# Saturating addition for the sampling coordinates of a deformable convolution, in place of an addition with a pointer scalar and a separate clip

## The chip, the cores and the metric

The kernel runs on one core of one Trainium2 chip. The core has five engines that work side by side, each from its own in-order list of instructions: TensorE (PE in the profile, with its weight loads as PEld), VectorE (DVE), ScalarE (ACT), GpSimd (POOL) and SyncE (SP), which here only starts DMA transfers. Engines wait for each other through semaphores. The metric is the time of one execution on the device in microseconds (us); lower is better. Before the change it is 9059.61 us, the median of three runs (9051.79, 9059.61 and 9065.78).

## What is computed

The input `x` is 16 images of 64 x 64 pixels with 128 channels. Layer 0 is a deformable sampling: a 3 x 3 convolution gives every channel and pixel two offsets, the offsets plus the pixel's own row and column are clipped to the image, and the normalized image is sampled there by bilinear interpolation. Layer 1 is an attention inside each token and a mixture of experts over 64 experts. Cut to the part that the change touches:

```python
offsets = conv(x, W) + b
off = offsets.transpose(0, 3, 1, 2).reshape(-1, h, w, 2)
coords = off.reshape(bc, -1, 2) + grid[None]
c0 = clip(coords[..., 0], 0, w - 1)
c1 = clip(coords[..., 1], 0, h - 1)
lt0, lt1, rb0, rb1 = floor(c0), floor(c1), ceil(c0), ceil(c1)
mapped = bilinear(xf, lt0, lt1, rb0, rb1, c0 - lt0, c1 - lt1)
```

## The kernel before

**Tiling.** An image is cut into eight chunks (`NCH`) of 8 columns x 64 rows, 512 pixels each. The 128 partitions hold channels. For a chunk the convolution runs on TensorE in two halves `s` (32 rows each), nine taps a half, into the PSUM tile `cbank` (128 x 512). For each half `coords(s)` turns the offsets in `cbank` into absolute coordinates in the SBUF tile `cd` (128 x 2 x 512: axis 0 is the row, axis 1 the column).

**From the coordinates to the sample.** `clip()` limits `cd` to 0..63, rounds the row coordinates to bfloat16 into `pc[:, 0]` on ScalarE, and sends the column coordinates to the DRAM buffer `cc_d` on SyncE's queue. `part2()` and `part3()` take the rounding's remainder twice (GpSimd and ScalarE), so that three bfloat16 numbers hold a row coordinate; `spread()` brings them by way of `pc_d` into the tile `parts`. All of this is for the next chunk. For the present chunk `sample()` takes two channels of each 32-channel group at a time (16 pairs `p` a chunk, each of two slots): `load_cols` broadcasts columns from `cc_d` into `chat` by DMA, `ramp_cols` makes a column weight of it on ScalarE, `spread_rows` broadcasts the row coordinates with bfloat16 matmuls into `yps` in PSUM, `ramp_rows` (ScalarE) makes `rhat` of it, `mains` multiplies with the image rows `xr` back into `yps`, `product` (VectorE) multiplies `yps` with `chat` into `prod`, and `sums` adds into `acc`. `tokens()` then runs a chunk's attention, whose large elementwise products (`sc`, `ev`) are on GpSimd, whose sums (`den`, `att`) are on VectorE, and whose exponentials are on ScalarE.

**Order.** Nothing is left to an automatic scheduler. `conv`, `sample`, `tokens`, `prep` and `tail` only record their operations with a slot (a due time; 32 slots a chunk). `Work.order()` then simulates the engines with the durations of `Work.duration()` and writes each engine's list: at every step, of the operations that are ready, the one with the smallest start plus 40 times its slot. `Work.duration()` charges a VectorE operation 145 ns + 1.045 ns an element + 30 ns for each pointer scalar, and a `tensor_scalar` from SBUF to SBUF 150 ns + 0.53 ns an element. [...] So a change in one operation's cost or kind alters the order of everything. `Work.emit()` (L200) issues the list; this is why almost all instructions carry line L204 in the profile, and why groups are told apart by the names of their tiles.

**Stages in time.** Image 0 runs alone; then a loop (L1271) of seven turns with two images each, whose work overlaps (while image b is sampled, the next one is normalized and the one before is finished); then image 15; then `general()`, which decides on a fallback for large offsets that these inputs don't take; then `finish()`, the experts and the output.

The two lines of `coords(s)` that make a coordinate, and the clip behind them:

```python
nc.vector.scalar_tensor_tensor(
    cd[:, 0], off[:, 0], cb, bcast(self.iot[:, 32 * s : 32 * (s + 1)], 2, SW),
    ALU.add, ALU.add)
...
nc.vector.tensor_scalar(self.cd, self.cd, 0.0, float(IMG - 1), ALU.max, ALU.min)
```

Here `cb` is a pointer scalar (one bias a partition) and `iot` a table 0..63. Behind the two coordinate operations of a half stands `far`, a reduction over the same `cbank`, after which TensorE may write `cbank` again.

Of the kernel before, what the change touches and what calls it, by code (L numbers as in the profile page):

```python
# [8 lines left out]

F32 = mybir.dt.float32  # L10
BF16 = mybir.dt.bfloat16
# [2 lines left out]
ALU = mybir.AluOpType  # L14
# [5 lines left out]
P = 128  # L20
B, IMG, C = 16, 64, 128
NPIX = IMG * IMG
NCH = 8
SW = IMG // NCH
# [23 lines left out]
def bcast(ap, axis, n):  # L48

    shape = list(ap.shape)  # L50
    return ap.unsqueeze(axis).to_broadcast(shape[:axis] + [n] + shape[axis:])
# [7 lines left out]
def by_columns(nc, out, weights, moving, start=True, stop=True):  # L59

    for c in range(0, out.shape[0], 32):
        nc.tensor.matmul(
            out[c : c + 32], weights[:, c : c + 32], moving, start=start, stop=stop)


def channel(t, v, m):

    a, h = divmod((v - m) % 4, 2)
    return 32 * m + 16 * a + 2 * t + h
# [87 lines left out]
class Work:  # L157
# [42 lines left out]
    def emit(self, ops):  # L200
        for op in ops:
            engine = getattr(self.nc, op.lane)
            for fn, args, kwargs in op.calls:
                getattr(engine, fn)(*args, **kwargs)  # L204

    def emit_in_order(self):
        self.emit(sorted(self.ops, key=lambda op: op.slot))
# [171 lines left out]
class Images:  # L379
# [8 lines left out]
    def __init__(self, ctx, tc, x, conv_w, conv_b, w_qkv, b_qkv, w_proj, b_proj, gate_w, gate_b,  # L388
# [3 lines left out]
        nc = tc.nc  # L392
# [30 lines left out]
        for v in range(4):  # L423
            for m in range(4):
                at, c = slice(32 * v + m, 32 * (v + 1), 4), channel(0, v, m)
                nc.scalar.dma_start(
                    self.cb[at], conv_b.rearrange("(c s) -> c s", s=2)[c : c + 15 : 2])
                for s in range(2):
                    engine = nc.vector if s else nc.gpsimd
# [44 lines left out]
        for r in range(2):  # L474
# [7 lines left out]
            for i, factor in enumerate((  # L482
# [3 lines left out]
        self.iot = keep([P, IMG], "iot")  # L486
        nc.gpsimd.iota(self.iot, [[1, IMG]], base=0, channel_multiplier=0,
                       allow_small_or_imprecise_dtypes=True)

# [10 lines left out]
        for g in range(4):  # L502
            for t in range(3):
                at = 32 * g + 8 * t
# [23 lines left out]
        for o in range(2):  # L528
# [5 lines left out]
            for g in range(4):  # L534
                for r in range(2):
                    at = 32 * g + 24 + r
# [31 lines left out]
        for m in range(4):  # L568
            nc.vector.memset(self.red[m], 0.0)
            for v in range(4):  # L570
                a, h = divmod((v - m) % 4, 2)
                at = 14 + 16 * a + h
# [211 lines left out]
    def conv(self, k, slot):  # L784
        plan = Work(self.nc, self.tc)
        nc = plan
        par, col = divmod(k, 4)

        def tap(s, t):
            kh, kw = divmod(t, 3)  # L790
            by_columns(
                nc, self.cbank, self.wconv[:, t, s, :],
                self.pad[:, kh + par : kh + par + 63 : 2, kw + 16 * col : kw + 16 * col + 16],
                start=(t == 0), stop=(t == 8))

        def coords(s):
            ps, hs = self.cbank, slice(256 * s, 256 * (s + 1))
            off = ps.rearrange("p (r w t) -> p t r w", w=SW, t=2)
            cd = self.cd[:, :, hs].rearrange("p t (r w) -> p t r w", w=SW)
            cb = self.cb[:, s : s + 1]  # L800
            nc.vector.scalar_tensor_tensor(
                cd[:, 0], off[:, 0], cb, bcast(self.iot[:, 32 * s : 32 * (s + 1)], 2, SW),
                ALU.add, ALU.add,
            )
            nc.vector.scalar_tensor_tensor(
                cd[:, 1], off[:, 1], cb, bcast(self.iot[:, SW * k : SW * (k + 1)], 1, 32),
                ALU.add, ALU.add,
            )
            nc.vector.tensor_reduce(
                self.far[:, 2 * k + s : 2 * k + s + 1], ps, AX.X, ALU.max,  # L810
                apply_absolute_value=True,
            )

        def clip():
            nc.vector.tensor_scalar(self.cd, self.cd, 0.0, float(IMG - 1), ALU.max, ALU.min)
            nc.scalar.copy(self.pc[:, 0], self.cd[:, 0])
            nc.sync.dma_start(self.cc_d[k % 2], self.cd[:, 1])

        def part2():
            nc.gpsimd.tensor_tensor(  # L820
                self.cd[:, 0], self.cd[:, 0], self.pc[:, 0], ALU.subtract)
            nc.scalar.copy(self.pc[:, 1], self.cd[:, 0])

        def part3():
            nc.gpsimd.tensor_tensor(
                self.pc[:, 2], self.cd[:, 0], self.pc[:, 1], ALU.subtract)

        def spread():
            for v in range(4):
                at = 32 * v  # L830
                nc.sync.dma_start(
                    self.pc_d[v].rearrange("o x n -> x o n"), self.pc[at : at + 32])
                nc.sync.dma_start(
                    self.parts[k % 2][at : at + 24].rearrange("p m n -> p (m n)"),
                    self.pc_d[v].rearrange("o (t m) n -> (o t) (m n)", t=8))


        for s, at in enumerate((range(5), range(12, 17))):
            for t in range(9):
                plan.together(slot + at[t // 2] + 0.5, lambda s=s, t=t: tap(s, t))  # L840
            plan.add(slot + at[-1] + 1, lambda s=s: coords(s))
        for i, fn in enumerate((clip, part2, part3, spread)):
            plan.add(slot + 18 + 2 * i, fn)
        return plan
# [640 lines left out]
```

## Time and profile before

The profile is of one execution, which took 9034.22 us by itself; its span (first to last instruction) is 9032.4 us, and 1.8 us lie around it. It is 0.28% below the median of the runs.

| what | value |
|---|---|
| median of three runs | 9059.61 us |
| the profiled execution's own time | 9034.22 us |
| its span | 9032.4 us |
| image 0, until the loop | 0 to 621 us |
| seven loop turns of two images | 621 to 7952 us, some 1047.8 us each |
| image 15 | 7952 to 8557 us |
| experts and output | 8557 to 9032 us |
| granted TensorE clock in the loop | 0.98 to 0.99 of full speed |
| coordinate additions (`cd<-cbank,cb,iot`) | 512 of 474 ns on VectorE |
| clips (`cd<-cd`) | 128 of 1002 ns on VectorE |

In the groups of instructions each row names the line, the engine, the operation, what it writes and reads, the shape and the count; behind the bar stand the busy time in us, the mean ns of one, and the idle time of the engine just before such instructions with what ended it. A row of the waits names who waited, for whom, the total us, how often, and the longest. A row of a stretch gives, for each engine, the busy us and, in brackets, the instructions.

### The profile page before, as it was taken

To read this page: it belongs to the slowest core of one execution; us is meant where nothing else is said; L and a number is where in the kernel's file an instruction comes from. 1 tells how busy PE (TensorE), PEld (TensorE's weight loads), DVE (VectorE), ACT (ScalarE), POOL (GpSimd) and SP (SyncE) were. 2 spreads that over 40 slices of the span, in tenths; PEclk is the share of its full clock that TensorE was granted. 3 is DMA by queue.
4 is the path that set the end of the run, shared out by engine and by line. 5 is a ranking of instruction groups with operands and counts; after the bars stand their busy time and mean duration, and the time that the engine had idled before them with its cause. 6 is when DMAs were issued, how large, how long until landed. Compare 5 with 4: busy or idle time off the path is not lost. (4 is left out here: it accounts for less than half of the span.)

```text
span 9032.4 us, 466631 instructions
## 1 busy us (share of the span) xinstructions
PE 8116.7 (90%) x205574; PEld 4234.7 (47%) x205574; DVE 7255.1 (80%) x10177; ACT 6550.6 (73%) x8082; POOL 7625.9 (84%) x5699
## 2 busy tenths in 40 slices
PE   6999999999999999999999999999999999999464
PEld 3544545454444545445454544445454544544234
DVE  3888888888888888888888888888878888888713
ACT  3777777777777878777777877778777877777400
POOL 1999998989999998989989899899989999899700
PEclk9999999999999999999999999999999999999656
DMA  5666666667666666667666766666676676666278
GB/s 140 189 180 182 192 183 184 191 187 194 176 188 177 194 184 191 186 179 197 181 185 180 196 191 179 184 179 193 181 195 181 184 198 175 185 177 185 78 238 295
DMA packets 1057495, 1678.72 MB, mean 186 GB/s; under 512 B 444272, under 2 KB 662128, under 8 KB 1051312
## 3 DMA queue, kind: packets, MB, share of 16 engines
q1 hardware_dynamic: 1033648, 1613.26, 63.9%
q8 instruction: 1615, 26.46, 1.3%
q10 hardware_dynamic: 21760, 35.14, 1.1%
q14 instruction: 472, 3.87, 0.2%
HBM read 1378.68 MB, written 268.96 MB: 182 GB/s over the span
## 5 line engine op out<-in xcount | busy, mean ns | idle before, releaser
L204 DVE SCALAR_TENSOR_TENSOR prod<-chat,yps 128x1024 f32<-128x1024 f32 x2048 | 2462.7, 1206 | 652.2 <-PE yps L204 142.0
L204 ACT ACTIVATE rhat<-yps 128x1024 f32<-128x1024 f32 x2048 | 2089.2, 1022 | 1153.8 <-PE yps L204 1004.6
L204 PEld LDWEIGHTS yps<-rhat,xr 32*32 32x32 f32 x131072 | 2174.8, 104 | 1385.3 <-ACT rhat L204 652.5
L204 PE MATMUL yps<-rhat,xr 32*32 32x176 f32 (+1 forms) x131072 | 2585.0, 275 | 199.6 <-ACT rhat L204 154.9
L204 POOL TENSOR_TENSOR ev<-sc,qkv 128x1024 f32<-128x1024 f32 x1019 | 2425.5, 2380 | 155.0 <-ACT sc L204 140.5
L204 PE MATMUL cbank<-pad,wconv 128*32 128x512 f32 x18432 | 2489.6, 617 | 49.1 <-DVE far L204 39.7
L204 POOL TENSOR_TENSOR sc<-qkv 128x1024 f32<-128x1024 f32 x1019 | 1980.1, 1943 | 46.3 <-POOLq L1271 7.5
L204 POOL TENSOR_TENSOR sc<-sc,top 128x1024 f32<-128x1024 f32 x1019 | 1993.7, 1958 | 20.2 <-ACT top L204 7.6
L204 DVE TENSOR_REDUCE den<-sc 128x64 f32<-128x1024 f32 x1024 | 1238.9, 1210 | 154.4 <-ACT sc L204 152.1
L204 ACT ACTIVATE chat<-chat,cbi,csc 128x1024 f32<-128x1024 f32 x1024 | 1265.0, 1239 | 108.7 <-DMA chat<-cc_d 100.1
L204 DVE TENSOR_REDUCE att<-ev 128x64 f32<-128x1024 f32 x1024 | 1237.3, 1208 | 103.3 <-POOL ev L204 73.9
L204 ACT ACTIVATE sc<-sc 128x1024 f32<-128x1024 f32 x1024 | 1078.1, 1053 | 198.6 <-POOL sc L204 149.1
L204 ACT ACTIVATE chat<-chat,cbi 128x1024 f32<-128x1024 f32 x1024 | 1159.0, 1142 | 25.0 <-DMA chat<-cc_d 23.7
L204 PE MATMUL acc<-prod,red 128*32 128x512 f32 x8192 | 1142.0, 617 | 20.7 <-DVE prod L204 19.2
L204 PE MATMUL yps<-parts,sel 32*32 32x512 bf16 x16384 | 926.2, 388 | 223.4 <-DVE prod L204 198.7
L204 PEld LDWEIGHTS cbank<-pad,wconv 128*32 128x32 f32 x18432 | 489.8, 109 | 891.9 <-issue 757.1
L204 PEld LDWEIGHTS <-sel 32*32 32x32 bf16 x16384 | 291.2, 88 | 1034.0 <-issue 993.4
L204 DVE RECIPROCAL den<-den 128x128 f32<-128x128 f32 x512 | 480.9, 939 | 7.7
L204 PE MATMUL bank<-wqkv,tr 128*32 128x384 f32 x4096 | 434.2, 495 | 17.1 <-DVE qkv L204 13.3
L204 DVE SCALAR_TENSOR_TENSOR qkv<-bank,rstd,bqkv 128x384 f32<-128x384 f32 x512 | 311.0, 607 | 108.5 <-PE bank L204 102.1
L204 POOL TENSOR_TENSOR att<-att,den 128x128 f32<-128x128 f32 x512 | 258.2, 504 | 120.7 <-DVE att L204 116.7
L204 POOL TENSOR_TENSOR qkv<-qkv,kmm 128x128 f32<-128x128 f32 x512 | 213.4, 417 | 157.9 <-DVE kmm L204 155.7
(166 smaller groups left out, 7629.2 us busy)
## 6 DMA issues: line engine op xcount, KB each, us to landing
chat<-cc_d SPq DMA_DIRECT2D x8192, 128.0 KB
xr<-xn_d SPq DMA_DIRECT2D x512, 128.0 KB
pc_d<-pc SPq DMA_DIRECT2D x512, 96.0 KB
parts<-pc_d SPq DMA_DIRECT2D x512, 96.0 KB
xl<-in_x_dram SPq DMA_DIRECT2D x128, 256.0 KB
xres<-in_x_dram SPq DMA_DIRECT2D x256, 128.0 KB
xn_d<-wt SPq DMA_DIRECT2D x128, 256.0 KB
cc_d<-cd SPq DMA_DIRECT2D x128, 256.0 KB
```

The source lines that it names most:

```text
L204: getattr(engine, fn)(*args, **kwargs)
```

## The change

A table `at` of grid plus bias is made once in the setup, one row of 64 for each of the two halves. A coordinate is then one operation: `cbank` plus the table, limited to 0..63 in the same instruction. [...] The clip is gone, and what followed it (the rounding to `pc`, the transfer to `cc_d`) now follows the coordinates directly. The planner knows the new call as `add_within` with two tensors and two constants, so it charges 145 ns + 1.045 ns an element and no pointer, and doesn't count it among the operations that it keeps apart from GpSimd's.

```diff
+                if fn == "add_within":
+                    out, a, b, lo, hi = args
+                    engine._custom_dve(TENSOR_ADD_SAT, out=out, in0=a, in1=b, s0=hi, s1=lo)
+                else:
+                    getattr(engine, fn)(*args, **kwargs)
...
+        self.at = keep([P, 2, IMG], "at")
+        for s in range(2):
+            nc.vector.tensor_scalar(
+                self.at[:, s], self.iot, self.cb[:, s : s + 1], None, ALU.add)
...
-            nc.vector.scalar_tensor_tensor(
-                cd[:, 0], off[:, 0], cb, bcast(self.iot[:, 32 * s : 32 * (s + 1)], 2, SW),
-                ALU.add, ALU.add,
-            )
-            nc.vector.scalar_tensor_tensor(
-                cd[:, 1], off[:, 1], cb, bcast(self.iot[:, SW * k : SW * (k + 1)], 1, 32),
-                ALU.add, ALU.add,
-            )
+            at = self.at[:, s]
+            for axis, grid in enumerate((
+                    bcast(at[:, 32 * s : 32 * (s + 1)], 2, SW),
+                    bcast(at[:, SW * k : SW * (k + 1)], 1, 32))):
+                nc.vector.add_within(cd[:, axis], off[:, axis], grid, 0.0, float(IMG - 1))
...
         def clip():
-            nc.vector.tensor_scalar(self.cd, self.cd, 0.0, float(IMG - 1), ALU.max, ALU.min)
             nc.scalar.copy(self.pc[:, 0], self.cd[:, 0])
             nc.sync.dma_start(self.cc_d[k % 2], self.cd[:, 1])
```

More of the change, by code (lines that the diff above doesn't have):

```diff
@@ L8 @@
 from concourse._compat import with_exitstack
+from concourse.dve_ops import TENSOR_ADD_SAT
 F32 = mybir.dt.float32
@@ L203, in emit @@
             for fn, args, kwargs in op.calls:
-                getattr(engine, fn)(*args, **kwargs)
+                if fn == "add_within":
[3 more added lines that the diff above has]
+                    getattr(engine, fn)(*args, **kwargs)
     def emit_in_order(self):
@@ L799, in coords @@
             cd = self.cd[:, :, hs].rearrange("p t (r w) -> p t r w", w=SW)
-            cb = self.cb[:, s : s + 1]
-            nc.vector.scalar_tensor_tensor(
-                cd[:, 0], off[:, 0], cb, bcast(self.iot[:, 32 * s : 32 * (s + 1)], 2, SW),
-                ALU.add, ALU.add,
-            )
-            nc.vector.scalar_tensor_tensor(
-                cd[:, 1], off[:, 1], cb, bcast(self.iot[:, SW * k : SW * (k + 1)], 1, 32),
-                ALU.add, ALU.add,
-            )
+            at = self.at[:, s]
[3 more added lines that the diff above has]
+                nc.vector.add_within(cd[:, axis], off[:, axis], grid, 0.0, float(IMG - 1))
             nc.vector.tensor_reduce(
```

## The prediction, made before the changed kernel ran

> **What bounds the kernel now.** I read the stretches first, one for each loop turn (second and third turn; the columns are PE, PEld, DVE, ACT and POOL busy, granted clock, DMA):
>
> ```profile
> 1669.00:2717.00 1048.00, 980.42 (x25508) 504.88 (x25504) 889.44 (x1240) 820.08 (x1013) 958.96 (x714) 0.98 0.67 187
> 2717.00:3764.00 1047.00, 979.64 (x25464) 505.04 (x25460) 887.23 (x1236) 814.61 (x1006) 953.48 (x710) 0.98 0.67 186
> ```
>
> PE is busy 93.5% of a turn, POOL 91%, DVE 85%. No engine is full: PE bounds, and loses 68 us of a turn to waits. Next the groups of PE in the turn from 1669 to 2717, for what ended those 68 us:
>
> ```profile
> L204 PE MATMUL yps<-rhat,xr 32*32 32x176 f32 (+1 forms) x16384 | 322.3, 275 | 24.8 <-ACT rhat L204 19.4 <-issue 4.5
> L204 PE MATMUL cbank<-pad,wconv 128*32 128x512 f32 x2324 | 315.2, 620 | 4.9 <-DVE far L204 4.7
> L204 PE MATMUL acc<-prod,red 128*32 128x512 f32 x1024 | 142.1, 616 | 2.2 <-DVE prod L204 2.2
> L204 PE MATMUL yps<-parts,sel 32*32 32x512 bf16 x2056 | 116.5, 388 | 27.3 <-DVE prod L204 24.6 <-PEq L1271 1.6 <-issue 0.7
> ```
>
> DVE ends 24.6 + 4.7 + 2.2 = 31.5 us of them. Third, DVE's groups, shapes kept apart:
>
> ```profile
> L204 DVE SCALAR_TENSOR_TENSOR prod<-chat,yps 128x1024 f32<-128x1024 f32 x2048 | 2462.7, 1206 | 652.2 <-PE yps L204 142.0 <-ACT sc L204 99.9 <-DMA chat<-cc_d 94.3
> ...
> L204 DVE SCALAR_TENSOR_TENSOR cd<-cbank,cb,iot 128x256 f32<-128x256 f32 x512 | 225.3, 474 | 87.3 <-PE cbank L204 87.1
> ...
> L204 DVE TENSOR_REDUCE far<-cbank 128x1 f32<-128x512 f32 x256 | 174.0, 680 | 0.0
> L204 DVE TENSOR_SCALAR cd<-cd 128x1024 f32<-128x1024 f32 x128 | 128.2, 1002 | 0.0
> ...
> L204 DVE TENSOR_TENSOR t<-bank,t 128x512 f32<-128x512 f32 x128 | 88.0, 688 | 85.0 <-PE bank L204 80.9 <-ACT sc L204 2.0 <-ACT chat L204 1.0
> ```
>
> The clip's mean of 1002 ns hides a spread, which the view of the tile `cd` gives (min/median/max), and the timeline around one clip shows why:
>
> ```profile
> L204 DVE TENSOR_SCALAR cd<-cd x128: 677/826/2769, 125.0 to 8367.5; 128x1024 f32<-128x1024 f32 x128
> ```
> ```profile
> 1584.14 2.38 POOL L204 TENSOR_TENSOR ev<-sc,qkv 128x1024 f32<-128x1024 f32 x1
> ...
> 1585.08 1.99 DVE L204 TENSOR_SCALAR cd<-cd 128x1024 f32<-128x1024 f32 x1
> ...
> 1586.48 0.85 POOL L204 TENSOR_TENSOR qkv<-qkv,kmm 128x128 f32<-128x128 f32 x1
> ```
>
> The clip begins beside POOL's `ev`, ends 0.55 us after it (1587.07 against 1586.52), and POOL's next instruction then takes 0.85 us where its group has 0.42: the two hold each other up.
>
> **Step 1, DVE's work.** The 128 clips go: 128.2 us, 16.0 in a turn. The 512 coordinate operations change kind. One of 512 elements reduced takes 680 ns, one of 1024 (`den`) 1210, so an element costs 1.035 ns and the 256 of `cd` 265; its fixed part is 474 - 265 = 209 ns. Without a pointer scalar the fixed part is 1206 - 1060 = 146 ns (`prod`) or 688 - 530 = 158 ns (`t`). The new operation should then take 411 to 423 ns; I take 417, 57 less, 29 us in all. This program of add, minimum and maximum is not in the trace. If it costs less than the rows say, I see no row under 411. Above stands RECIPROCAL, 939 ns for 128 elements, about 6.2 ns an element, which would make 1.74 us. MAX8 and MATCH_REPLACE8 (4411 and 4398 ns for 4096) and the batch-norm statistics (685 for 512) run about one element in 1.04 ns, so I go by those. The two operations for `at` (190 ns each by the `mats` row, 64 elements) fall near 15.6 us, before DVE idles 5.93 us for a transfer: nothing. DVE is freed of 128 + 29 = 157 us, 2.2% of 7255.
>
> **Step 2, POOL's work.** Sorting POOL's instructions by whether a clip ran beside them: 66 `att` take 763 ns against 466; 56 of `sc<-sc,top` 2197 against 1944; 23 of `sc<-qkv` 2069 against 1940; 7 of `qkv` 856 against 411. That is 19.6 + 14.2 + 3.0 + 3.1 = 40 us, 5 in a turn. The new operation reads PSUM and one SBUF table, as the old addition did, beside which I see no such lengthening.
>
> **Step 3, what reaches the end.** Low: the order stays as good and only work on the chain counts. I followed the chain back through six turns (from the last matmul, at idle time to the releaser, else to the instruction before). DVE is 16% of it, POOL 2.5%, the coordinate additions 8.1 us a turn, the clip never. 57/474 of 8.1 is 1.0 us. Of 423 waits of PE and PEld that DVE ended in seven turns, 14 had a clip in DVE's unbroken work before them, at most 8.4 us, so up to 1.2 a turn; half of it, 0.6, makes 1.6 a turn. With 16 images as eight turns: 13 us. High: queueing. DVE's busy share falls from 84.9% to 83.0%; if waiting goes as busy over free, 5.62 becomes 4.88, 13% less, 4.1 us of the 31.5, 33 us in eight turns, plus the 8 us of pointers: 41. Between: 27 us.
>
> **Step 4, what moves.** The instruction order of the changed kernel shows DVE's loop body at 1225 instead of 1241 instructions, PE's at the same work in another order. Cover on PE, as work by the rows' durations: between `mains` and the next `spread_rows` on the same `yps` median 2.4 us in both; between `spread_rows` and `mains` 1.54 and 1.55; between one half's last tap and the next half's first 4.2 before, 4.9 after. So no step loses its cover. SP's transfer to `cc_d` moves up past 2 to 21 `chat` loads, `parts` up to 7, the rounding on ACT 0 to 5 pairs, POOL's two remainders stay within a group. A new order has a price of either sign: the two images of a turn are the same work in two orders, and between the reductions `most` lie 519.5 and 526.8 us, the latter with 3.8 us of PE idle at the loop's edge. That leaves 3.5 us, 0.7%; for a mean of two, 0.5%: 45 us either way.
>
> [...] The removed wait of POOL is a row (763 against 466). [...]
>
> **Rivals.** (a) The relief goes further: DVE's lateness also stands behind the ramps (19.4 us a turn) and POOL's waits; a third of 31.5 goes, 10 us a turn: 80 us, 8980. (b) Nothing arrives: the clip is off the chain, PE's waits stay: 4 us or less, 9056. (c) Slower: SP is an in-order queue, and now stands at `cc_d` sooner, behind coordinates that DVE may do late, while `chat` loads queue behind it. For and against:
>
> ```profile
> SPq L204 <- DVE cd L204: 115.6, 90, 11.0
> ```
> ```profile
> ACT chat L204 <- DMA chat<-cc_d: 123.8, 141, 3.3
> ```
>
> SP waits here already, and late `chat` costs ACT 123.8 and DVE 94.3 us, 218 in all. If these rise by half, 109 us, and half of it reaches PE: 55 - 27 = 28 us slower, 9088. It decides from a rise of a quarter (54 us). Against it: the clip that went was part of SP's wait. (d) The new operation is dear: at two cycles an element 150 + 530 = 680 ns, the chain's 8.1 us grow by 3.5 a turn, 28 us, against 19 of the rest: 9069. It turns from 612 ns (19/65 over 474). At RECIPROCAL's rate it would be past 9200. That the clip isn't removed is excluded: the order has none.
>
> **How the numbers follow.** From the profiled 9034.2 the sum gives 9007; the median of the runs stands 25.4 us above it, so 9059.6 - 27 = 9033. A difference under 0.2% (18 us) can't be told from none. Chances: forecast 0.45, with its own spread 9005 to 9041; (a) 0.14; (b) 0.22; (c) 0.13; (d) 0.06, of which 0.01 at RECIPROCAL's rate. Faster 0.59, same 0.22, slower 0.19. The range reaches to (a) with the new order's spread and to (c), 8965 to 9095; the dearest end of (d) is left out.
>
> **What would show it.** Step 1: additions near 417 ns, DVE some 157 us lower. Step 2: `att` near 466 ns, POOL some 40 us lower. Step 3: PE's idle time in a turn from 68 to about 65 us, the waits on `prod` lower. For (c): SP's and ACT's waits for `cd` and `chat` higher. For (d): additions over 600 ns. I am wrong if the new order's own luck exceeds 45 us, or if PE's matmuls themselves change.

## The result: 0.31% slower

The changed kernel takes 9081.03 us (median of 9 runs, 9070.88 to 9090.23), the kernel before, run beside it, 9052.07 (9 runs, 9035.34 to 9065.78). The ratio is 1.0031, 95% interval 1.0021 to 1.0041: some 28 us slower, where 27 us faster was forecast. The profiled execution took 9082.71 us, 2.0 us above its span of 9080.7.

What was priced as an instruction of the change came out as priced. First the groups of DVE in the changed kernel, shapes kept apart (busy us, mean ns of one, idle before):

```profile
L209 DVE SCALAR_TENSOR_TENSOR prod<-chat,yps 128x1024 f32<-128x1024 f32 x2048 | 2464.5, 1207 | 738.1 <-PE yps L209 169.5 <-ACT chat L209 132.2 <-ACT xln L209 87.3
...
L207 DVE CUSTOM_DVE_ANT_1 cd<-cbank,at 128x256 f32<-128x256 f32 x512 | 196.9, 415 | 79.1 <-PE cbank L209 70.3 <-issue 8.4
...
L209 DVE TENSOR_REDUCE far<-cbank 128x1 f32<-128x512 f32 x256 | 174.1, 680 | 0.0
L209 DVE SCALAR_TENSOR_TENSOR big<-big,logits 64x512 f32<-64x512 f32 x128 | 128.9, 1058 | 0.8 <-ACT logits L209 0.6
...
L209 DVE TENSOR_TENSOR gmv<-gmv 128x1 f32<-128x1 f32 x32 | 50.5, 1579 | 1.3
L209 DVE TENSOR_TENSOR farthest<-farthest,most 128x1 f32<-128x1 f32 x16 | 28.6, 1786 | 0.5
```

The saturating addition takes 415 ns (forecast 411 to 423), there is no clip, and DVE's idle time before `prod` grew. But DVE's busy time fell by 78 us only, from 7255.1 to 7176.8, not by 157. Three rows (`big`, `gmv`, `farthest`) took part of it back, against these of the kernel before, which the prediction did not look at:

```profile
L204 DVE SCALAR_TENSOR_TENSOR big<-big,logits 64x512 f32<-64x512 f32 x128 | 108.2, 880 | 0.8 <-ACT logits L204 0.6
...
L204 DVE TENSOR_TENSOR gmv<-gmv 128x1 f32<-128x1 f32 x32 | 21.5, 673 | 1.1
L204 DVE TENSOR_TENSOR farthest<-farthest,most 128x1 f32<-128x1 f32 x16 | 18.6, 1166 | 0.5
```

20.7 + 29.0 + 10.0 = 60 us more, for the same instructions. The two `gmv` operations have one element a partition and belong to the group normalization of the next image (`group3`); they have two SBUF operands, and their durations range from 159 to 2065 ns.

Second, the stretches, as before one for a loop turn (PE, PEld, DVE, ACT, POOL, clock, DMA), of the changed kernel:

```profile
2725.00:3780.00 1055.00, 985.65 (x25472) 505.48 (x25472) 880.29 (x1221) 816.61 (x1008) 949.38 (x710) 0.98 0.67 185
3780.00:4835.00 1055.00, 986.02 (x25472) 506.86 (x25472) 879.49 (x1221) 816.63 (x1008) 948.91 (x711) 0.98 0.67 185
```

From the loop's branches a turn takes 1053.5 us, 1046.6 before (means of the last six turns; the 1047.8 above is 1 us too long): 6.9 us more. All seven turns together are 55 us longer, image 0 is 5.4 us shorter and what follows the loop 1.7, which makes the 48 us between the two profiled executions, so the loss lies in the loop alone. (Some 20 of these 48 us are the spread of runs: the medians are 29 us apart, and the profiled execution of before lies 18 under its median.) POOL's busy time in a turn is 6 us lower and DVE's 8, and both only wait longer. PE idles 70.0 us a turn, 67.5 before, and its busy time grew by 4.4 us with the same matmuls in another order.

Third, the groups of PE by what ended their idle time, over the six turns from 1674 to 7995 of the changed kernel:

```profile
L209 PE MATMUL yps<-rhat,xr 32*32 32x176 f32 (+1 forms) x98304 | 1927.8, 275 | 161.2 <-ACT rhat L209 136.8 <-issue 17.1
L209 PE MATMUL cbank<-pad,wconv 128*32 128x512 f32 x13824 | 1863.3, 618 | 18.0 <-DVE far L209 10.4 <-DVE prod L209 3.9 <-issue 3.4
...
L209 PE MATMUL yps<-parts,sel 32*32 32x512 bf16 x12288 | 708.6, 390 | 167.2 <-DVE prod L209 144.0 <-issue 10.8 <-PEq L1275 8.2
...
L209 PE MATMUL bank<-gmv,avg 128*32 128x2 f32 (+1 forms) x192 | 6.0, 184 | 33.0 <-DVE gmv L209 33.0
```

and of the kernel before, six turns from 1669 to 7945:

```profile
L204 PE MATMUL cbank<-pad,wconv 128*32 128x512 f32 x13824 | 1871.3, 618 | 30.4 <-DVE far L204 28.6 <-issue 0.5
...
L204 PE MATMUL bank<-gmv,avg 128*32 128x2 f32 (+1 forms) x192 | 5.7, 178 | 8.2 <-DVE gmv L204 8.2
```

The wait for `far` fell from 28.6 to 10.4 us. The wait for `gmv` rose from 8.2 to 33.0 and took back more than that. The timeline of the changed kernel around one `gmv` shows how:

```profile
1547.84 2.34 POOL L209 TENSOR_TENSOR ev<-sc,qkv 128x1024 f32<-128x1024 f32 x1
...
1548.77 3.32 DVE L209 TENSOR_TENSOR gmv<-gmv 128x1 f32<-128x1 f32 x2
1550.15 1.92 POOL L209 TENSOR_TENSOR sc<-sc,top 128x1024 f32<-128x1024 f32 x1
1552.01 1.21 DVE L209 SCALAR_TENSOR_TENSOR prod<-chat,yps 128x1024 f32<-128x1024 f32 x1
1552.14 0.29 PE L209 MATMUL bank<-gmv,avg 128*32 128x1 f32 x8 [3.71 <-DVE gmv L209]
```

Two operations of one element hold DVE for 3.32 us: the first takes 1431 ns and ends at 1550.20, 0.02 us after `ev` on POOL (1550.18), the second 1853 ns and ends at 1552.09, 0.02 us after `sc` (1552.07). PE stands 3.71 us, `prod` is late behind them, and PE then waits for it too. In the kernel before `gmv` falls beside `ev` as well, but late in it, and POOL's next instruction is a short one:

```profile
1539.95 2.38 POOL L204 TENSOR_TENSOR ev<-sc,qkv 128x1024 f32<-128x1024 f32 x1
...
1541.69 1.01 DVE L204 TENSOR_TENSOR gmv<-gmv 128x1 f32<-128x1 f32 x2
...
1542.27 0.41 POOL L204 TENSOR_TENSOR qkv<-qkv,kmm 128x128 f32<-128x128 f32 x1
...
1542.75 0.24 PE L204 MATMUL bank<-gmv,avg 128*32 128x1 f32 x8 [0.23 <-DVE gmv L204]
```

There the same two operations take 1.01 us, and PE stands 0.23.

### The profile page after: what moved, and what is told of

Its sections match the earlier page's. It is cut to its first block, busy times and chain, and to the rows that moved or that the text cites. A ratio compares the mean times of both kernels' runs of the same rounds, so it can differ in the third digit from the quotient of the medians.

```text
span 9080.7 us, 466361 instructions
## 1 busy us (share of the span) xinstructions
PE 8151.2 (90%) x205574; PEld 4237.7 (47%) x205574; DVE 7176.8 (79%) x10051; ACT 6552.8 (72%) x8082; POOL 7579.2 (83%) x5699
## 5 line engine op out<-in xcount | busy, mean ns | idle before, releaser
L209 PE MATMUL bank<-wqkv,tr 128*32 128x384 f32 x4096 | 440.9, 503 | 15.0 <-DVE qkv L209 12.6
L209 PEld LDWEIGHTS acc<-prod,red 128*32 128x32 f32 x8192 | 183.2, 109 | 321.5 <-issue 283.6
```

## The experiments

The theory after this reading: **the instructions gain, the new order loses.** Any change of a cost makes the planner write another order for all engines, and in this one the `gmv` operations fall where they wait for two long GpSimd instructions in a row. The rival: the new instruction, or the clip's absence, costs by itself. Ratios below are to the kernel before, run in the same batch, with 95% intervals.

**New instructions in the old order.** The planner sees the old operations; only what is issued differs. The lists of PE, ACT, POOL and SP are the same as before, one for one.

```diff
+                if "instead" in kwargs:
+                    kwargs["instead"](engine)
...
             nc.vector.scalar_tensor_tensor(
                 cd[:, 0], off[:, 0], cb, bcast(self.iot[:, 32 * s : 32 * (s + 1)], 2, SW),
                 ALU.add, ALU.add,
+                instead=sat(0, bcast(at[:, 32 * s : 32 * (s + 1)], 2, SW)),
...
-            nc.vector.tensor_scalar(self.cd, self.cd, 0.0, float(IMG - 1), ALU.max, ALU.min)
+            nc.vector.tensor_scalar(self.cd, self.cd, 0.0, float(IMG - 1), ALU.max, ALU.min,
+                                    instead=lambda engine: None)
```

> The order of every engine's list is that of the kernel before; only the coordinate operations are the saturating additions, and the clip is dropped from the list. Theory 'order' (the instructions save, the new order loses more): 5 to 40 us faster than before, so about 9012 to 9047. Rival 'instructions' (the saturating addition or the missing clip is what costs): slower than before by some 20 to 40 us, like the changed kernel. Rival 'nothing' (the clip was off the chain): within 5 us of before.

Measured 9036.15 against 9048.86 us: 0.9986 (0.9975 to 0.9997), 12.7 us faster. The rival falls: in this order the saturating addition and the missing clip together cost nothing. The new order then costs 1.0031 / 0.9986 = 1.0045, about 41 us. In this run DVE's busy time fell by 132 us (7255.1 to 7123.0). PE's wait for `far`, over six turns, stayed near the 28.6 us of before, so its fall to 10.4 in the changed kernel is the new order's and not that of the cheaper coordinates:

```profile
L208 PE MATMUL cbank<-pad,wconv 128*32 128x512 f32 x13824 | 1868.6, 615 | 30.6 <-DVE far L208 25.1 <-ACT pad L208 3.6 <-issue 2.0
```

**Old instructions in the new order**, the clip right behind a chunk's fourth addition:

```diff
-                    engine._custom_dve(TENSOR_ADD_SAT, out=out, in0=a, in1=b, s0=hi, s1=lo)
+                    cb, iot, whole = kwargs["old"]
+                    engine.scalar_tensor_tensor(out, a, cb, iot, ALU.add, ALU.add)
+                    if whole is not None:
+                        engine.tensor_scalar(whole, whole, lo, hi, ALU.max, ALU.min)
```

> The order of every engine's list is that of the changed kernel, but the coordinates are made by the old additions with a pointer, and the clip stands right behind the fourth of a chunk. Theory 'order': slower than the changed kernel by the 5 to 40 us that the instructions save, so 9086 to 9120. Rival 'instructions': as before, about 9052, or faster.

9213.56 us, 1.0177 (1.0161 to 1.0194): worse than either theory said, 1.46% above the changed kernel. My place for the clip was part of it. The tile `cd` of this run, and who waited:

```profile
L210 DVE TENSOR_SCALAR cd<-cd x128: 693/1513/2467, 123.0 to 8521.5; 128x1024 f32<-128x1024 f32 x128
```
```profile
PEld cbank L212 <- DVE far L212: 83.3, 56, 5.0
```

The clip, 1513 ns in the median here (826 in the kernel before), stood ahead of `far` and so kept `cbank` from PE; in the changed kernel that wait is 28.7 us. So a second form has it behind `far` (`old` is given with the `far` of a chunk's second half):

```diff
+                    if old is not None:
+                        engine.tensor_scalar(old[0], old[0], 0.0, float(IMG - 1), ALU.max, ALU.min)
```

> The order of the changed kernel, the old additions with a pointer, and the clip behind the reduction far of a chunk's second half, where it does not hold cbank. With the clip ahead of far it was 1.45% slower than the changed kernel. Theory 'the list has no room for the clip': still 0.5 to 1.2% slower than the changed kernel, ratio to before 1.008 to 1.015, with SP and ScalarE waiting for the clip. Rival 'only cbank was held': ratio 1.003 to 1.006.

9168.03 against 9062.88 us: 1.0105 (1.0084 to 1.0125). That is still 0.7% above the changed kernel. So taking the clip and the pointers out is worth 0.14% in an order made for them and 0.7% in one made without: an order fits its own list of operations, though the place for the clip was still chosen by hand and not by the planner.

**The two `gmv` operations mended.** In the changed kernel's order, they take their second operand as a pointer scalar:

```diff
-            nc.vector.tensor_tensor(gmv[:, 0:1], gmv[:, 0:1], gmv[:, 2:3], ALU.subtract)
-            nc.vector.tensor_tensor(gmv[:, 1:2], gmv[:, 0:1], gmv[:, 0:1], ALU.mult)
+            nc.vector.tensor_scalar(gmv[:, 0:1], gmv[:, 0:1], gmv[:, 2:3], None, ALU.subtract)
+            nc.vector.tensor_scalar(gmv[:, 1:2], gmv[:, 0:1], gmv[:, 0:1], None, ALU.mult)
```

(written this way here; in the runs only the issue differs, and the planner sees the old form.)

> The changed kernel with its order; only the two one-element subtractions and squarings of gmv in the group normalization are written with a pointer scalar instead of two SBUF tensors, which in the changed kernel took 1579 ns each against 673 before. If these waits for GpSimd are a large part of the loss (TensorE waited 33.0 us for gmv in six turns against 8.2): about 30 us faster than the changed kernel, 9050. If TensorE only waits elsewhere instead: within 8 us of 9081.

9010.08 us, 0.9954 (0.9940 to 0.9968): 0.77% under the changed kernel, some 70 us, more than expected. The same operation in the tile `gmv` of the changed kernel and of this run (min/median/max ns):

```profile
L209 DVE TENSOR_TENSOR gmv<-gmv x32: 159/1662/2065, 94.7 to 7872.7; 128x1 f32<-128x1 f32 x32
```
```profile
L210 DVE TENSOR_SCALAR gmv<-gmv x32: 212/214/216, 93.6 to 7794.8; 128x1 f32<-128x1 f32 x32
```

and the timeline of this run, where `gmv` again falls beside `ev`:

```profile
1530.91 2.35 POOL L212 TENSOR_TENSOR ev<-sc,qkv 128x1024 f32<-128x1024 f32 x1
...
1531.83 0.46 DVE L210 TENSOR_SCALAR gmv<-gmv 128x1 f32<-128x1 f32 x2
...
1532.35 0.24 PE L212 MATMUL bank<-gmv,avg 128*32 128x1 f32 x8 [0.84 <-DVE gmv L210]
```

With a pointer scalar the pair takes 0.46 us beside the same GpSimd instruction. With two tensors, in the changed kernel, one operation took 159 ns with no GpSimd instruction beside it and up to 2065 ns with one, so one element a partition is enough for that; with the pointer scalar it took 212 to 216 ns in all 32 cases of this run.

**The same in the kernel before, and in both together.**

> The kernel before with its order; only the two one-element operations of gmv are written with a pointer scalar, as in the run of the changed kernel that went to 9010. There they took 1579 ns, here 673 on average, so by the same measure (71 us for 1579 - 214) some 24 us faster than before: 9025. Theory 'the loss of the changed kernel is the place of gmv': before stays some 10 to 30 us above 9010, so that without the gmv waits the change is a gain. Rival 'gmv costs both alike': 9010 or lower, and the change is no gain even then.

> The order of the kernel before, the saturating additions in it with the clip dropped, and gmv with a pointer scalar. If the two savings add (13 us for the instructions, some 24 for gmv): 9012. If the freed time only lands at the next wait: 9025 to 9036.

Kernel before with `gmv` mended: 0.9981 (0.9972 to 0.9989). Old order, new instructions and `gmv` mended: 0.9973 (0.9961 to 0.9985). So with `gmv` out of the way the changed kernel is at 0.9954 and the kernel before at 0.9981, 0.27% in favour of the change; with it, 0.31% against. In the old order the two savings almost add (0.9986 x 0.9981 = 0.9967). And the same instructions with `gmv` mended are at 0.9954 in the new order and at 0.9973 in the old: mending takes 0.77% off in the new order and 0.13% in the old. The new order, 0.45% dearer with these waits, costs nothing without them, which shows that they are its price.

**Another small wait of the same kind**, in the changed kernel with `gmv` mended: the maximum `farthest`, issued with a pointer scalar too (again in the issue alone).

```diff
-        nc.vector.tensor_tensor(self.farthest, self.farthest, far, ALU.max)
+        nc.vector.tensor_scalar(self.farthest, self.farthest, far, None, ALU.max)
```

> The changed kernel with its order and gmv with a pointer scalar, and also the one-element maximum farthest (1786 ns for each of 16 images) with a pointer scalar. If every wait of DVE for GpSimd passes on as the ones of gmv did (71 us for 2.7 us an image): 16 x 1.57 us and more, so 8965 to 8990. If it passes on only where TensorE waits behind it, as theory says of gmv alone: within 10 us of 9010.

0.9958 (0.9945 to 0.9971) against 0.9954 without it: no gain. The 1.57 us an image that DVE lost there, 25 in all, passed to nobody, and the changed kernel's trace shows no engine that waits for `farthest`. So what costs is not the wait itself, but PE's being behind it.

**Other orders.** Is the loss the change's, or this order's? The same two kernels were planned with other weights of a slot (40 is the original):

```diff
-HASTE = 40
+HASTE = 42
```

> The kernel before with the planner's weight of a slot (HASTE) at 42 instead of 40: the same instructions in another order. Theory 'order' says that a new order alone moves the time by some tenths of a per cent in either direction: 9005 to 9100, and likely more than 9 us from 9052. If orders of this planner are all alike: within 9 us of before.

> The changed kernel with the planner's weight of a slot at 42 instead of 40: the same instructions in another order. Theory 'the loss is this order's luck': 9000 to 9075, below 9081. Rival 'any order of the changed kernel is slow': 9075 or more. The kernel before went to 9066 with 42.

> The kernel before in its other order (weight 42) with gmv by a pointer scalar; there gmv took 581 ns, so some 10 to 20 us less than the 1.0015 it had: ratio 0.997 to 1.001 to before.

> The changed kernel in its other order (weight of a slot 42) with gmv by a pointer scalar. With the gmv waits gone the change should be a gain in this pair of orders too: 0.2 to 0.4% under the kernel before in the same other order with gmv mended, which runs beside it. If the other loss of this order is not gmv (there gmv takes 955 ns, TensorE waits 19.5 us for it): above that kernel.

> The kernel before, planned with a weight of 38 for a slot. Theory 'order': anywhere within 0.4% of before (0.996 to 1.004), more than 0.1% off as likely as not.

> The changed kernel, planned with a weight of 38. If the loss belongs to the change: 0.2 to 0.4% slower than the kernel before at 38. If it was the order: between 0.4% faster and 0.4% slower than that, and slower by more than 0.2% only where gmv takes well over 700 ns.

In its simulation the planner keeps a VectorE operation that reads two SBUF operands of more than one element, and a `tensor_scalar` or a copy from SBUF to SBUF, from running beside a GpSimd operation (`Work.shared()`). The same two kernels with a planner that does so for a `tensor_tensor` on two SBUF tensors of one element too:

```diff
-            wide = [a for a in given if a.space == SBUF and a.free_size() > 1]
+            wide = [a for a in given if a.space == SBUF
+                    and (a.free_size() > 1 or fn == "tensor_tensor")]
```

> The kernel before, whose planner keeps additions and products of two SBUF tensors apart from GpSimd even where they have one element. gmv should fall to some 160 to 350 ns from 673, worth about what mending gmv was (0.19%): ratio 0.996 to 1.000, plus or minus 0.3% for the new order.

> The changed kernel with the same planner. gmv should fall to some 160 to 350 ns from 1579; if the planner's ignorance was the cause, 0.3 to 0.8% faster than the changed kernel: ratio 0.995 to 1.000 to before, and not above the kernel before with this planner by over 0.2%.

| order | kernel before | changed kernel | changed over before | mean ns of `gmv`, before and changed |
|---|---|---|---|---|
| weight 40 | 1 | 1.0031 (1.0021 to 1.0041) | +0.31% | 673, 1579 |
| weight 42 | 1.0015 (1.0006 to 1.0024) | 1.0036 (1.0023 to 1.0050) | +0.21% | 581, 955 |
| weight 38 | 1.0094 (1.0072 to 1.0116) | 1.0053 (1.0032 to 1.0073) | -0.41% | 760, 615 |
| planner knows | 1.0034 (1.0019 to 1.0048) | 0.9985 (0.9971 to 0.9998) | -0.49% | 219, 1042 |
| weight 40, `gmv` mended | 0.9981 (0.9972 to 0.9989) | 0.9954 (0.9940 to 0.9968) | -0.27% | 214, 214 |
| weight 42, `gmv` mended | 1.0014 (1.0001 to 1.0026) | 1.0011 (0.9999 to 1.0023) | -0.03% | 211, 193 |

The sign goes either way, so the loss belongs to the order and not to the change. Orders of one and the same kernel lie 0.9% apart (kernel before, 1 to 1.0094). `gmv` got longer with the change in three of the four orders; in two of them the change lost, and mending `gmv` took 0.58% off the difference at weight 40 and 0.24% at weight 42 (from 0.21 to -0.03; this one hardly clear of noise). In the third, with the planner that knows, it gained: there `gmv` takes 1042 ns, but PE's waits for it before `bank` are 9.1 us in the whole run, 42.9 in the changed kernel at weight 40. And `gmv` is not the whole of an order's price: the slowest kernel of the table, the one before at 38, has it at 760 ns only, and the planner that was told of it wrote the kernel before a slower order.

Several of these expectations missed. The kernel before at 38 was to lie within 0.4% and lies 0.9% off; with the planner that knows it was to gain from `gmv` and lost 0.34%, and `gmv` in the changed kernel did not fall to 160 to 350 ns; at weight 42 mending `gmv` gave it nothing (1.0015 to 1.0014), and the changed kernel was to be 0.2 to 0.4% under it and is level. The changed kernel at 42 lies inside its range in us (9069.54), but the kernel before ran at 9033.83 beside it; by the ratio it is no better than at 40, as the rival had it, and only the last two orders rule that rival out.

**One part alone**, in the old order: the coordinates by a plain addition from the table, the clip kept (the cut is against the first run above).

```diff
-                return lambda engine: engine._custom_dve(
-                    TENSOR_ADD_SAT, out=cd[:, axis], in0=off[:, axis], in1=grid,
-                    s0=float(IMG - 1), s1=0.0)
+                return lambda engine: engine.tensor_tensor(
+                    cd[:, axis], off[:, axis], grid, ALU.add)
```

> One part of the change alone, in the order of the kernel before: the coordinates by a plain addition from the table without a pointer, 512 x about 57 ns of VectorE less, and the clip stays. The prediction's chain gave 8 us for it; with saturating addition and clip dropped the same order gained 13 us (0.9986). So a ratio of 0.999, or nothing that can be told.

0.9988 (0.9976 to 1.0001): as expected in size, but not told from nothing, nor from the whole change's 0.9986 in that order. How the 13 us divide between pointer and clip stays open. The plain addition took 415 ns, as the saturating one does.

## Why the prediction was wrong

**Bound and step 1, right in their prices, short by the returns.** PE bounds with waits. The addition went from 474 to 415 ns; the 128 us of clips went. What the step left out is that of DVE's 157 us some 60 came back in the new order as longer times of `big`, `gmv` and `farthest` beside GpSimd (`big` takes 685 ns at most with no GpSimd instruction beside it, in the changed kernel up to 2868 with one); in the old order 132 of the 157 arrived. So the load of an engine some of whose instructions get longer beside another engine's isn't the sum of its rows.

**Step 2, right.** `att` takes 467 ns (forecast 466), and POOL's busy time fell by 47 us (forecast 40). POOL waited longer in their place.

**Step 3, its low end right in number, not shown in mechanism.** In a fixed order the gain is 12.7 us (2.7 to 22.6 by the interval); the chain and the counted waits gave 13, the queueing estimate 41. The middle of the two was a choice that nothing in the trace backed: the row that said that the clip is never on the chain should have decided. But the way was not the forecast one: with the new instructions in the old order PE's waits for `prod` and `far` are 12.6 us lower over six turns, 2.1 a turn, while others rose, and PE's idle time in a turn is 67.9 us against 67.5. That the sum met the time so closely is partly luck.

**Step 4 failed.** It said "no step loses its cover" and put the new order at 45 us either way with a middle of nothing. The new order cost 41 us (by the two runs in the old and the new order), more than the gain, so the sign of the forecast hung on it, and the forecast left that to the width of the range. That 41 lies within 45 is in part luck: at weight 38 the kernel before lies 85 us from itself. The cover was counted for three of PE's waits only: `mains`, `spread_rows` and the taps. The fourth, PE on the group normalization, was in the rows (`gmv` 673 ns on average, 159 at its fastest), and the new order moved it: 33.0 us of PE's idle time in six turns instead of 8.2.

**The rivals.** (a) and (b) are out by the result. (c), slower through SP, ended on the right side for a wrong reason. The changed kernel's waits:

```profile
SPq L209 <- DVE cd L207: 99.6, 62, 9.3
```
```profile
ACT chat L209 <- DMA chat<-cc_d: 106.7, 138, 3.3
```

Both are lower than before (115.6 and 123.8). In the old order, without the clip, SP's wait fell to 24.6 us but ACT's rose to 132.6, so the one does not bring the other. (d) is out with 415 ns.

**The clock behind a wait.** Mending `gmv` gave 70 us, and its operations became only 2.7 us an image shorter, 44 in all. The traces show the other part. A turn became 9.7 us shorter, 6.2 of it PE's idle time and 3.5 its busy time, and the busy time goes with the granted clock. This is the stretch ahead of the `gmv` in the timeline above and the one at it (columns as before; the clock, third from the end, is 1.00 and then 0.50):

```profile
1540.00:1550.00 10.00, 8.44 (x196) 3.35 (x188) 7.83 (x10) 8.31 (x10) 9.92 (x7) 1.00 0.61 159
1551.00:1557.00 6.00, 4.01 (x37) 1.04 (x38) 5.86 (x7) 2.99 (x3) 3.41 (x6) 0.50 0.34 111
```

In the clock records of the 18 traces the clock is either full or half, and of PE's waits in the loop 174 of the 177 over 3.5 us have a half-clock stretch begin within them or in the 3 us behind (7 of 7 in the kernel before, 14 of 14 in the changed kernel), 468 of the 930 from 1.5 to 2.5 us, and 406 of the 2408 from 0.9 to 1.5. Inside such stretches of the changed kernel's loop a `cbank` matmul takes 1061 ns, outside 608 (medians). They fill 35.3 us of a turn in the kernel before, 43.2 in the changed kernel and 37.0 with `gmv` mended; half of the difference, 4.0 and 3.1 us, is nearly all by which PE's busy time rose (4.4) and fell (3.5). So a long wait of PE cost more than its length here. At weight 42 PE's waits for `gmv` before `bank` are, in the kernel before and in the changed one:

```profile
PE bank L204 <- DVE gmv L204: 21.0, 29, 1.9
```
```profile
PE bank L209 <- DVE gmv L209: 21.0, 14, 2.7
```

The sum is the same, but in the changed kernel's loop these are seven waits of 2.7 us, each with half clock at it or behind it, in the kernel before fourteen of 1.0 us at most. Mending `gmv` was worth 0.25% in the one and 0.01% in the other, which fits, though that difference is hardly clear of noise.

**What stays open.** PE's busy time in a turn differs by some 8 us between orders (978 to 986 us, without the two runs that put the clip back). Less half of the half-clock time it is 961 to 965 us in all 18 traces, so most of this is the clock; which waits bring it about in each order, beyond `gmv`, is not traced, and neither is why the order at weight 38 is the slowest.

## What to carry to other kernels

In a kernel whose order a planner writes, an edit has two prices: that of its instructions, measured with the old order held fixed, and that of the new order, which is a draw (here 0.9% between the best and the worst of four orders of one kernel). When the first is smaller than the second, as with an operation off the chain of waits, plan the two kernels in several orders before believing a sign. And look for the cheapest operations with the widest spread of durations (159 to 2065 ns for one element): where TensorE stands behind them, they can be worth more than the long ones; the changed kernel with these two issued by a pointer scalar beats both kernels, at 0.9954.

## What was not expected of the hardware

A VectorE operation on one element a partition, with both operands in SBUF, took 159 ns alone and up to 2065 ns beside a GpSimd instruction (changed kernel); two in a row beside two GpSimd instructions took 3.32 us. With a pointer scalar in place of the second tensor it took 212 to 216 ns in all 32 cases. The saturating addition (`CUSTOM_DVE_ANT_1`) took 415 ns for 256 elements from PSUM and SBUF, as did the plain addition of the same two operands; with a pointer scalar the old addition took 474, some 60 more, and `gmv` 214 against 159 alone. Within or just behind waits of PE over 3.5 us the granted clock fell to half in 174 of 177 cases; of all half-clock stretches in the loop, 35 of 43 in the kernel before and 62 of 64 in the changed kernel are 3.4 or 6.8 us long.
